# First block of a graph convolution ahead of the others, later loads on another queue, source scores from one vector, and the softmax of two target blocks ahead of the rest

## Chip, cores and metric

One core of a Trainium2 chip runs the whole program. The metric is device time in microseconds (us): the median of the runs of one kernel. The engines are named as in the profile: PE (TensorE), DVE (VectorE), ACT (ScalarE), POOL (GpSimd), and SP (SyncE), which here only issues transfers.

## What is computed

Four graph layers run one after the other on 3,125 nodes with 256 features and 100,000 edges; after each, the result is added to x and normalized by row. The change touches the first two:

```python
x = _layernorm(x + _L0_gnn_ref(x, edge_index, L0_gnn_W1, L0_gnn_W2))
x = _layernorm(x + _L1_gnn_ref(x, edge_index, edge_attr_128, Wn, bn, We, be, attn))
# layer 0, gcn_conv(x, W1), relu, gcn_conv(h, W2):
h = x @ W;  deg = segment_sum(ones, dst);  dinv = where(deg > 0, rsqrt(deg), 0)
return segment_sum(h[src] * (dinv[src] * dinv[dst])[:, None], dst)
# layer 1, attention over the edges of each target:
h = x @ Wn.T + bn;  e = edge_attr @ We.T + be
a = leaky_relu(sum((h[src] + e) * attn), 0.01)
a = exp(a - segment_max(a, dst)[dst]);  a = a / (segment_sum(a, dst)[dst] + 1e-16)
return relu(segment_sum(h[src] * a[:, None], dst))
```

Layers 2 and 3 are a gated graph layer and another convolution with a small decoder. The program works in float32; where bfloat16 is used, a float32 value is split into three bfloat16 parts.

## The kernel before

Nodes lie in 25 blocks of 128 rows (NBK). Every gather and scatter is a matrix product: for a target block b and a source block s a 128x128 "slab" holds the weights of the edges between them, and the output of b is the sum over s of slab times features. A slab is itself a product of one-hot matrices. Edges stand in a table sorted by (target block, source block, half of the target rows), up to 128 in a tile, 50 tiles for one target block (TS).

The stages, with the rows of the profile that they have:

- **Records.** dense_path first works out a row for every edge and scatters 784 groups of 128 records into the table in DRAM, with indirect DMAs on POOL's queue (L498). A record has the packed rows of source and target, two edge weights, and the edge's share of the attention score (the features times a vector made of We and attn). At the end of this stage the features H0 = dinv * (x @ W1) are split into three bfloat16 parts (L337 to L343).
- **First convolution** (pool "layer0"). For each block, load_records loads the block's records on SP (L809, tile rec_b, three buffers), casts them to source and target keys on DVE (L813 to L820), and copies the score share into q on ACT (L821). Two halves of 13 and 12 source blocks follow: onehot makes the one-hots os and od on DVE (L729), build_slab multiplies them on PE (L755) and ACT evacuates four slabs at a time (L756, PSUM in three buffers) into the bfloat16 tile wo (four buffers). apply_parts does 75 matmuls (L775). ACT scales and rectifies the sum (L838), project multiplies by W2 (two transposes L680, evacuation L681, matmuls L687), ACT scales (L841), and split writes three parts into H1 (L712 and L715 on ACT, L714 and L716 on DVE). Each slab is also written to DRAM on SP (L835).
- **Second convolution and scores.** Ten transposes turn the keys round (L850, L852), and ten writes put them into DRAM (L853). Then, for each block b: its slab is loaded on SP (L803), applied to H1 (L775), added to x with dinv (L883), normalized (norm: L696 to L704, a square root on ACT at L702), multiplied by WnT (project), bn is added to give H (L886), and the source score s1 of each node is the sum of H * attn_r over the features, plus a constant kc (L888 to L890); it is split into three parts (s1p). scores(b - 1) reads keys of the edges with that source block, broadcast to all rows (L868), compares them with the row number (L869), looks the scores up by 50 small matmuls (L871), adds them to q and takes the leaky rectifier (L874 to L877).
- **Attention.** From all of q the largest value in each target block is found: reduce (L940), transpose (L932), reduce (L934), broadcast by a matmul (L943); it is subtracted (L944) and the exponential taken (L945). For each target block weights_split splits q into three parts (L899 to L903), weighted multiplies them into the one-hots od (L909), build_slab and apply_f32 follow (L755, L783). bounds tests the spread of the scores for a flag and runs behind block 0.
- Layers 2 and 3 follow with the same helpers.

In the stages named here no order is written out by hand: a scheduler puts the instructions of each engine in an order by their place in the program, raised by a priority where one is given, and each engine then runs its own in that order. Loads of x, W2, WnT, bn and attn_r are issued from ACT's queue (L657, L666, L671); the loads of records and slabs and the writes of slabs from SP's.

Of the kernel before, what the change touches and what calls it, by code (L numbers as in the profile page):

```python
# [8 lines left out]
F32 = mybir.dt.float32  # L9
# [3 lines left out]
OP = mybir.AluOpType  # L13
# [56 lines left out]
def in_pairs(ap):  # L70

    return ap.rearrange("p n (c two) -> p n c two", two=2)
# [27 lines left out]
def dense_path(ctx: ExitStack, tc: tile.TileContext, a: dict, out: bass.AP, flag: bass.AP):  # L100
# [553 lines left out]
    nc.gpsimd.memset(x1[:, :, 0], 1.0)  # L654
    nc.gpsimd.memset(x1[:, :, D + 1], 1.0)
    x = x1[:, :, 1:D + 1]
    nc.scalar.dma_start(x, a["x_rows"])  # L657
    stats = keep.tile([P, NBK, 2], F32, name="stats")
    rstd = keep.tile([P, NBK], F32, name="rstd")
    s1 = keep.tile([P, NBK], F32, name="s1")  # L660


    def weight(pool, v, name):
        k, m = v.shape
        t = pool.tile([P, k // P, m], F32, name=name)
# [44 lines left out]
    def split(dst, src, shape):  # L710

        nc.scalar.activation(dst[0], src, AF.Copy)  # L712
        r = wk.tile(shape, F32, name="split")
        nc.vector.tensor_tensor(r, src, dst[0], op=OP.subtract)  # L714
        nc.scalar.activation(dst[1], r, AF.Copy)  # L715
        nc.vector.tensor_tensor(dst[2], r, dst[1], op=OP.subtract)  # L716

    oh = ctx.enter_context(tc.tile_pool(name="d_oh", bufs=2))

# [4 lines left out]
    until1 = ctx.enter_context(ExitStack())  # L724
    q = until1.enter_context(tc.tile_pool(name="d_q", bufs=1)).tile([P, NT], F32, name="q")

    def onehot(k, n, name, cols=P):
        t = halfslab(name, cols=cols)
        nc.vector.tensor_tensor(in_pairs(t[:, :n, :]), repeat(iota_b[:, :cols], n), pair(k, cols), op=OP.is_equal)  # L729
        return t  # L730

    def half_slabs():
# [73 lines left out]
    def load_records(b):  # L806
        ts = slice(b * TS, (b + 1) * TS)
        r = wk.tile([P, TS, 4], F32, name="rec_b", bufs=3)
        load = nc.sync.dma_start(r, trows[:, ts, :])  # L809
        for name in done:  # L810
            tc.add_manual_dep(load.ins, name, DATA, reason="it reads rows of all scatters")
        both = wk.tile([P, TS], I32, name="both")
        nc.vector.tensor_copy(both, r[:, :, 0])  # L813
# [7 lines left out]
        nc.scalar.activation(q[:, ts], r[:, :, 3], AF.Copy)  # L821


    s1p = keep.tile([P, NBK, 3], BF, name="s1p")
    with tc.tile_pool(name="layer0", bufs=1) as pool:
        W2 = weight(pool, a["L0_gnn_W2"], "W2")
        H1 = pool.tile([P, NBK, 3, D], BF, name="H1")
        for b in range(NBK):
            load_records(b)
            slab = halfslab("wo", 4)[:, :NBK, :]  # L830
            for o, n in half_slabs():
                os = onehot(cut(keys, b, o, n), n * TB, "os")
                od = onehot(cut(keyd, b, o, n), n * TB, "od", HP)
                build_slab(slab[:, o:o + n, :], b, o, n, os, [od], True)
# [3 lines left out]
            nc.scalar.activation(y, p, AF.Relu, scale=dinv[:, b:b + 1])  # L838
# [40 lines left out]
        for b in range(NBK):  # L879
            p = apply_parts(load_slab(b), H1, D)  # L880
            if b:
                scores(b - 1)
            nc.vector.scalar_tensor_tensor(x[:, b, :], p, dinv[:, b:b + 1], x[:, b, :], op0=OP.mult, op1=OP.add)  # L883
            norm(b)
            p = project(x[:, b, :], WnT, D)
            nc.vector.tensor_add(H[:, b, :D], p, bn)  # L886
            m = wk.tile([P, D], F32, name="tmp")
            nc.vector.tensor_tensor(m, H[:, b, :D], attn_r, op=OP.mult)  # L888
            nc.vector.tensor_reduce(s1[:, b:b + 1], m, axis=AX.X, op=OP.add)
            nc.vector.tensor_scalar(s1[:, b:b + 1], s1[:, b:b + 1], kc, None, op0=OP.add)  # L890
            split([s1p[:, b, i:i + 1] for i in range(3)], s1[:, b:b + 1], [P, 1])
        scores(NBK - 1)

    def weights_split(dst, tmp, w, n, bufs=1):

# [7 lines left out]
        nc.vector.tensor_copy(dst[:, 2], tw(lo))  # L903

    def weighted(oh, w3, n):
        r = []
# [19 lines left out]
    with tc.tile_pool(name="layer1", bufs=2) as pool:  # L926
        den = pool.tile([P, NBK], F32, name="den", bufs=1)

        def largest(v, n=1):

            vt = psT.tile([P, P], F32, name="tp")
            nc.tensor.transpose(vt[:n, :], v, ident)  # L932
            r = pool.tile([n, 1], F32, name=f"largest{n}", bufs=6)
            nc.vector.tensor_reduce(r, vt[:n, :], axis=AX.X, op=OP.max)  # L934
            return r
# [4 lines left out]
        nc.vector.tensor_reduce(bmax, q_by_target, axis=AX.X, op=OP.max)  # L940
        r = largest(bmax, NBK)
        c = psT.tile([P, NBK], F32, name="tp")
        nc.tensor.matmul(c, r.to_broadcast([NBK, P]), ident[:NBK, :NBK], start=True, stop=True)  # L943
        nc.vector.tensor_tensor(q_by_target, q_by_target, c[:, :, None].to_broadcast([P, NBK, TS]), op=OP.subtract)  # L944
# [885 lines left out]
```

## Time and profile before

| | us |
|---|---|
| median of 3 runs | 3448.73 |
| lowest and highest run | 3438.39 and 3451.22 |
| profiled execution, time | 3273.78 |
| profiled execution, span | 3271.9 |
| PE busy in the span | 2550.6 (78%) |
| DVE busy | 2232.4 (68%) |
| ACT busy | 921.8 (28%) |
| POOL busy | 789.0 (24%) |

The span goes from the first to the last instruction of one execution. Busy shares are means over stages with different limits; a stage is read from its own stretch of the timeline. In a row of the timeline stand start, duration, engine, line, operation, output and inputs, and the count; in brackets, how long the engine had been idle and what ended that.

### The profile page before, as it was taken

How to read it: one execution, taken by the hardware profiler on the slowest of the kernel's cores; microseconds unless marked ns; L12 is line 12 of the kernel's file. 1: busy time of each engine (PE TensorE's matmuls, PEld its weight loads, DVE VectorE, ACT ScalarE, POOL GpSimd, SP SyncE). 2: the span in 40 equal slices, each digit the busy share in tenths (PEclk: the TensorE clock that was granted, in tenths of full speed). 3: DMA queues.
4: the chain of work that ended last, by engine and by line, in shares of the span. 5: the costliest groups of instructions: out<-in, count | busy, mean ns of one | idle time of the engine just before them, and what ended most of it. 6: DMA issues, size and time to landing. Idle time of an engine off the chain costs nothing.

```text
span 3271.9 us, 60046 instructions
## 1 busy us (share of the span) xinstructions
PE 2550.6 (78%) x25737; PEld 1964.7 (60%) x25737; DVE 2232.4 (68%) x3824; ACT 921.8 (28%) x1827; POOL 789.0 (24%) x874
## 2 busy tenths in 40 slices
PE   4544443333520999999979999999999999999998
PEld 2222222222310888788868888888888767767754
DVE  8997766666773655355578888666666767767545
ACT  3332222222221444200022222222222334334321
POOL 4777777777775000000000000000000000000000
PEclk6555566666555999999989999999999999999999
DMA  4222222222212211465400000100001010010143
GB/s 138 81 78 65 70 71 71 71 71 62 79 30 59 99 72 78 165 231 217 182 2 2 2 2 2 44 15 16 16 13 19 10 13 10 10 13 9 45 138 118
DMA packets 171989, 203.46 MB, mean 62 GB/s; under 512 B 119719, under 2 KB 144796, under 8 KB 165441
## 3 DMA queue, kind: packets, MB, share of 16 engines
q1 hardware_dynamic: 134698, 188.26, 18.0%
q10 hardware_dynamic: 11927, 9.63, 1.0%
q0 software_dynamic: 25088, 1.66, 0.8%
q8 instruction: 203, 3.33, 0.4%
q14 instruction: 73, 0.60, 0.1%
HBM read 167.60 MB, written 31.86 MB: 61 GB/s over the span
## 4 chain that ended last, share of the span: by engine, by line
PE 51%; POOL 18%; DVE 17%; issue 7%; ACT 5%; DMA 2%; ACTq 0%; DVEq 0%; POOLq 0%; SPq 0%
PE acc L783 18%; POOL table L498 18%; PE acc L775 11%; PE mm L687 6%; PE slab L755 5%; DVE wo L909 4%; PE acc L1156 3%; DVE os L729 3%; PE tp L680 2%; DVE eq L465 1%; ACT L1112 1%; PE look L871 1%; ACT xT L681 1%; DVE od L729 1%; DVE rank L469 1%
## 5 line engine op out<-in xcount | busy, mean ns | idle before, releaser
L498 POOL DMA_INDIRECT table<-rec,row x784 | 757.2, 966 | 263.7 <-issue 216.9
L783 PE MATMUL acc<-x,slab_f 128*128 128x257 f32 x2500 | 592.5, 386 | 0.0
L909 DVE TENSOR_TENSOR wo<-od,w 128x1664 bf16<-128x1664 bf16 (+1 forms) x450 | 434.0, 984 | 134.8 <-PE slab L755 108.5
L783 PEld LDWEIGHTS acc<-x,slab_f 128*128 128x128 f32 x2500 | 455.8, 189 | 71.4 <-issue 5.9
L361 PE MATMUL place<-by_target,op 128*128 128x100 bf16 x392 | 40.7, 281 | 460.5 <-ACT tick L512 419.7
L775 PEld LDWEIGHTS <-wo 128*128 128x128 bf16 x3750 | 363.9, 98 | 47.9 <-issue 3.1
L755 PEld LDWEIGHTS <-os 128*128 128x128 bf16 x8750 | 296.8, 98 | 109.3 <-ACT q L821 61.4
L729 DVE TENSOR_TENSOR os<-iota_b,keys 128x3328 bf16<-128x3328 bf16 (+1 forms) x150 | 272.9, 1819 | 115.3 <-PE slab L755 114.2
L361 PEld LDWEIGHTS <-op 128*128 128x128 bf16 x392 | 33.7, 135 | 463.5 <-issue 285.3
L783 PE MATMUL acc<-features,slab_f 128*128 128x257 f32 x1250 | 297.1, 388 | 0.0
L755 PE MATMUL slab<-wo,os 128*128 128x64 bf16 x7500 | 261.1, 193 | 13.4 <-ACT slab_f L756 8.2
L783 PEld LDWEIGHTS acc<-features,slab_f 128*128 128x128 f32 x1250 | 227.9, 190 | 43.3 <-issue 12.1
L756 ACT ACTIVATE slab_f<-slab 128x512 f32<-128x512 f32 (+1 forms) x350 | 182.6, 549 | 146.0 <-PE slab L755 140.9
L775 PE MATMUL acc<-H,wo 128*128 128x256 bf16 x1875 | 218.9, 273 | 0.0
L775 PE MATMUL acc<-features,wo 128*128 128x256 bf16 x1875 | 212.9, 274 | 0.0
L1038 POOL COPY keys_t<-keys 128x2500 bf16<-128x2500 bf16 x1 | 2.5, 2520 | 721.2 <-ACT tmp L975 721.2
L512 ACT ACTIVATE tick<-place 1x1 f32<-1x1 f32 x48 | 7.7, 160 | 533.0 <-POOL tock L513 500.0
L465 DVE TENSOR_SCALAR eq<-gap 128x512 bf16<-128x512 f32 x196 | 121.8, 682 | 39.4 <-PE gap L439 39.4
L729 DVE TENSOR_TENSOR od<-iota_b,keyd 128x1664 bf16<-128x1664 bf16 (+1 forms) x150 | 147.6, 984 | 0.0
L767 PEld LDWEIGHTS <-wo 128*64 128x64 bf16 x3750 | 112.0, 110 | 47.5 <-issue 47.5
L420 PEld LDWEIGHTS <-by_target 128*52 128x52 bf16 x784 | 90.6, 138 | 77.3 <-issue 49.0
L767 PE MATMUL slab<-os,wo 128*64 128x128 bf16 x3750 | 129.6, 220 | 4.7 <-ACT slab_f L769 4.7
(286 smaller groups left out, 3621.7 us busy)
## 6 DMA issues: line engine op xcount, KB each, us to landing
ea<-in_edge_attr SPq DMA_DIRECT2D x49, 1024.0 KB
wo<-slabs SPq DMA_DIRECT2D x50, 800.0 KB
os<-rows SPq DMA_DIRECT2D x25, 832.0 KB
slabs<-wo SPq DMA_DIRECT2D x25, 800.0 KB
od<-rows SPq DMA_DIRECT2D x25, 768.0 KB
table<-rec,row POOLq DMA_INDIRECT x784, 2.1
dr<-db_row SPq DMA_DIRECT2D x48, 208.0 KB
rec_b<-table SPq DMA_DIRECT2D x75, 100.0 KB
```

Source lines behind the costliest of these rows:

```text
L420: nc.tensor.matmul(cnt[:, c + 1:, :], it["by_target"][:, c], it["by_source"][:, c:c + 1, :].to_broadcast([P, CH - c, KB]), start=False, st ...
L465: nc.vector.tensor_scalar(eq[:, 4 * g:4 * g + 4, :], of[k]["gap"][g], 0.0, None, op0=OP.is_equal)
L498: i = nc.gpsimd.indirect_dma_start(out=table, out_offset=bass.IndirectOffsetOnAxis(ap=ready[k][:, c:c + 1], axis=0), in_=rec[:, k * CH + c ...
L687: nc.tensor.matmul(p[:, :m], l, r, start=(i == 0), stop=(i == len(w) - 1))
L729: nc.vector.tensor_tensor(in_pairs(t[:, :n, :]), repeat(iota_b[:, :cols], n), pair(k, cols), op=OP.is_equal)
L755: nc.tensor.matmul(p[:, i - g, own], l, r, start=(m == 0), stop=(m == len(terms) - 1))
L756: nc.scalar.activation(dst[:, g:g + w, :], p[:, :w, :], AF.Copy)
L767: nc.tensor.matmul(p[j * HP:(j + 1) * HP, i - g, :], stat[:, i * TB + j, :], mov[:, i * TB + j, :], start=(m == 0), stop=(m == len(stats) ...
L775: nc.tensor.matmul(p[:, :m], slab[:, s, :], parts[:, s, k, :m], start=(s == 0 and k == 0), stop=(s == NBK - 1 and k == 2))
L783: nc.tensor.matmul(p[:, :m], t[:, s, :], H[:, o + s, :m], start=(o + s == 0), stop=(o + s == NBK - 1))
L909: nc.vector.tensor_tensor(in_pairs(t[:, :n, :]), in_pairs(oh[:, :n, :]), pair(w3[k], HP), op=OP.mult)
L1156: nc.tensor.matmul(acc[b][:, :3 * F0], slab[b][:, s, :], H3[:, s].rearrange("p k m -> p (k m)"), start=(s == 0), stop=(s == NBK - 1))
```

## The change

- The first block of the first convolution gets a high priority, so that the scheduler takes its records, one-hots and slab ahead of the other blocks'. The copy of the score share into q goes from ACT to POOL.
- The loads of x, WnT, bn and attn_r move from ACT's queue, at the start of the stage, to SP's queue behind block 2; that of W2 to SP's queue behind the first block's slab.
- The source score is no longer taken from H: a vector v = WnT times attn, brought to all rows (v_row), and a constant c_row = bn . attn + kc are made once; s1 is then the sum of x * v_row, plus c_row. H is made as before, but its product comes behind the score in the program.
- The last block's score and its lookup get a high priority, and its H comes behind them in the program.
- The softmax is done in two parts, target blocks 0 and 1 with a high priority, and 2 to 24 behind block 0's slabs in the program. The largest value is still that of each target block.
- Four dependencies, handed out by onehot from the list behind, make the first four one-hots of attention wait: the first for the last block's split score, the second for the first part's reduction, the next two for block 0's split weights.

```diff
-    nc.scalar.dma_start(x, a["x_rows"])
...
-    def weight(pool, v, name):
+    def weight(pool, v, name, q=nc.scalar):
...
-        nc.scalar.dma_start(t, v.rearrange("(k p) m -> p k m", p=P))
+        q.dma_start(t, v.rearrange("(k p) m -> p k m", p=P))
...
+    behind = []
+
     def onehot(k, n, name, cols=P):
         t = halfslab(name, cols=cols)
-        nc.vector.tensor_tensor(in_pairs(t[:, :n, :]), repeat(iota_b[:, :cols], n), pair(k, cols), op=OP.is_equal)
+        i = nc.vector.tensor_tensor(in_pairs(t[:, :n, :]), repeat(iota_b[:, :cols], n), pair(k, cols), op=OP.is_equal)
+        if behind:
+            tc.add_manual_dep(i.ins, behind.pop(0).ins.name, DATA, reason="what others wait for comes first")
         return t
...
-        nc.scalar.activation(q[:, ts], r[:, :, 3], AF.Copy)
+        nc.gpsimd.tensor_copy(q[:, ts], r[:, :, 3])
...
+    SOON = 20000
     with tc.tile_pool(name="layer0", bufs=1) as pool:
-        W2 = weight(pool, a["L0_gnn_W2"], "W2")
         H1 = pool.tile([P, NBK, 3, D], BF, name="H1")
         for b in range(NBK):
-            load_records(b)
...
+            with tc.high_priority(0 if b else 20000):
+                load_records(b)
+                slab = halfslab("wo", 4)[:, :NBK, :]
+                for o, n in half_slabs():
...
+                    build_slab(slab[:, o:o + n, :], b, o, n, os, [od], True)
+            if b == 0:
+                W2 = weight(pool, a["L0_gnn_W2"], "W2", nc.sync)
...
+            if b == 2:
+                WnT = pool.tile([P, KD, D], F32, name="WnT")
+                bn, attn_r = [pool.tile([P, D], F32, name=n) for n in ("bn", "attn_r")]
+                for t, v in ((x, a["x_rows"]), (WnT, a["WnT"].rearrange("(k p) m -> p k m", p=P)), (bn, row_bcast(a["L1_gnn_bn"])),
+                             (attn_r, row_bcast(a["L1_gnn_attn"].rearrange("o h c -> (o h c)")))):
+                    tc.keep_in_program_order(nc.sync.dma_start(t, v))
...
-        WnT, bn = weight(pool, a["WnT"], "WnT"), bias(pool, a["L1_gnn_bn"], "bn")
-        attn_r = bias(pool, a["L1_gnn_attn"].rearrange("o h c -> (o h c)"), "attn_r")
...
+        vc = pool.tile([P, KD], F32, name="vc")
+        for k in range(KD):
+            m = wk.tile([P, D], F32, name="tmp")
+            nc.vector.tensor_tensor(m, WnT[:, k, :], attn_r, op=OP.mult)
+            nc.vector.tensor_reduce(vc[:, k:k + 1], m, axis=AX.X, op=OP.add)
+        m = wk.tile([P, D], F32, name="tmp")
+        nc.vector.tensor_tensor(m, bn, attn_r, op=OP.mult)
+        c_row = pool.tile([P, 1], F32, name="c_row")
+        nc.vector.tensor_reduce(c_row, m, axis=AX.X, op=OP.add)
+        nc.vector.tensor_scalar(c_row, c_row, kc, None, op0=OP.add)
+        p = psM.tile([P, 512], F32, name="mm")
+        for k in range(KD):
+            nc.tensor.matmul(p[:, k * P:(k + 1) * P], vc[:, k:k + 1].to_broadcast([P, P]), ident, start=True, stop=True)
+        v_row = pool.tile([P, D], F32, name="v_row")
+        nc.scalar.activation(v_row, p[:, :D], AF.Copy)
...
-            nc.vector.scalar_tensor_tensor(x[:, b, :], p, dinv[:, b:b + 1], x[:, b, :], op0=OP.mult, op1=OP.add)
-            norm(b)
-            p = project(x[:, b, :], WnT, D)
-            nc.vector.tensor_add(H[:, b, :D], p, bn)
-            m = wk.tile([P, D], F32, name="tmp")
-            nc.vector.tensor_tensor(m, H[:, b, :D], attn_r, op=OP.mult)
-            nc.vector.tensor_reduce(s1[:, b:b + 1], m, axis=AX.X, op=OP.add)
-            nc.vector.tensor_scalar(s1[:, b:b + 1], s1[:, b:b + 1], kc, None, op0=OP.add)
-            split([s1p[:, b, i:i + 1] for i in range(3)], s1[:, b:b + 1], [P, 1])
-        scores(NBK - 1)
+            with tc.high_priority(SOON if b == NBK - 1 else 0):
+                nc.vector.scalar_tensor_tensor(x[:, b, :], p, dinv[:, b:b + 1], x[:, b, :], op0=OP.mult, op1=OP.add)
+                norm(b)
+                m = wk.tile([P, D], F32, name="tmp")
+                nc.vector.tensor_tensor(m, x[:, b, :], v_row, op=OP.mult)
+                nc.vector.tensor_reduce(s1[:, b:b + 1], m, axis=AX.X, op=OP.add)
+                nc.vector.tensor_scalar(s1[:, b:b + 1], s1[:, b:b + 1], c_row, None, op0=OP.add)
+                parted = split([s1p[:, b, i:i + 1] for i in range(3)], s1[:, b:b + 1], [P, 1])
+            if b < NBK - 1:
+                p = project(x[:, b, :], WnT, D)
+                nc.vector.tensor_add(H[:, b, :D], p, bn)
+        with tc.high_priority(SOON):
+            scores(NBK - 1)
+        p = project(x[:, NBK - 1, :], WnT, D)
+        nc.vector.tensor_add(H[:, NBK - 1, :D], p, bn)
...
-        nc.vector.tensor_reduce(bmax, q_by_target, axis=AX.X, op=OP.max)
-        r = largest(bmax, NBK)
-        c = psT.tile([P, NBK], F32, name="tp")
-        nc.tensor.matmul(c, r.to_broadcast([NBK, P]), ident[:NBK, :NBK], start=True, stop=True)
-        nc.vector.tensor_tensor(q_by_target, q_by_target, c[:, :, None].to_broadcast([P, NBK, TS]), op=OP.subtract)
-        nc.scalar.activation(q, q, AF.Exp)
+        def softmax(d0, d1):
+            qs, n = q_by_target[:, d0:d1, :], d1 - d0
+            i = nc.vector.tensor_reduce(bmax[:, d0:d1], qs, axis=AX.X, op=OP.max)
+            r = largest(bmax[:, d0:d1], n)
+            c = psT.tile([P, NBK], F32, name="tp")
+            nc.tensor.matmul(c[:, :n], r.to_broadcast([n, P]), ident[:n, :n], start=True, stop=True)
+            nc.vector.tensor_tensor(qs, qs, c[:, :n, None].to_broadcast([P, n, TS]), op=OP.subtract)
+            nc.scalar.activation(qs, qs, AF.Exp)
+            return i
+
+        with tc.high_priority(SOON):
+            i = softmax(0, 2)
+        behind += [parted, i]
...
-            weights_split(w3, wk, q[:, b * TS:(b + 1) * TS], TS, 2)
+            i = weights_split(w3, wk, q[:, b * TS:(b + 1) * TS], TS, 2)
+            if b == 0:
+                behind += [i, i]
             slab = weighted_slab(pool, b, keys, keyd, w3)
+            if b == 0:
+                softmax(2, NBK)
```

More of the change, by code (lines that the diff above doesn't have):

```diff
@@ L715, in split @@
         nc.scalar.activation(dst[1], r, AF.Copy)
-        nc.vector.tensor_tensor(dst[2], r, dst[1], op=OP.subtract)
+        return nc.vector.tensor_tensor(dst[2], r, dst[1], op=OP.subtract)
     oh = ctx.enter_context(tc.tile_pool(name="d_oh", bufs=2))
@@ L820, in load_records @@
             nc.vector.tensor_copy(k[:, ts, :], t[:, :, None].to_broadcast([P, TS, 2]))
-        nc.scalar.activation(q[:, ts], r[:, :, 3], AF.Copy)
+        nc.gpsimd.tensor_copy(q[:, ts], r[:, :, 3])
+    SOON = 20000
     s1p = keep.tile([P, NBK, 3], BF, name="s1p")
     with tc.tile_pool(name="layer0", bufs=1) as pool:
-        W2 = weight(pool, a["L0_gnn_W2"], "W2")
         H1 = pool.tile([P, NBK, 3, D], BF, name="H1")
         for b in range(NBK):
-            load_records(b)
[L830 to L834, printed above, removed]
+            with tc.high_priority(0 if b else 20000):
+                load_records(b)
+                slab = halfslab("wo", 4)[:, :NBK, :]
+                for o, n in half_slabs():
+                    os = onehot(cut(keys, b, o, n), n * TB, "os")
+                    od = onehot(cut(keyd, b, o, n), n * TB, "od", HP)
+                    build_slab(slab[:, o:o + n, :], b, o, n, os, [od], True)
+            if b == 0:
+                W2 = weight(pool, a["L0_gnn_W2"], "W2", nc.sync)
             nc.sync.dma_start(slabs[b].rearrange("p (s d) -> p s d", d=P), slab)
@@ L902, in weights_split @@
         nc.vector.tensor_tensor(lo, hi, dst[:, 1, :, 0], op=OP.subtract)
-        nc.vector.tensor_copy(dst[:, 2], tw(lo))
+        return nc.vector.tensor_copy(dst[:, 2], tw(lo))
     def weighted(oh, w3, n):
@@ L933, in largest @@
             r = pool.tile([n, 1], F32, name=f"largest{n}", bufs=6)
-            nc.vector.tensor_reduce(r, vt[:n, :], axis=AX.X, op=OP.max)
-            return r
+            nc.vector.tensor_reduce(r[:n], vt[:n, :], axis=AX.X, op=OP.max)
+            return r[:n]
         bmax = pool.tile([P, NBK], F32, name="bmax", bufs=1)
         q_by_target = q.rearrange("p (d t) -> p d t", d=NBK)
-        nc.vector.tensor_reduce(bmax, q_by_target, axis=AX.X, op=OP.max)
-        r = largest(bmax, NBK)
-        c = psT.tile([P, NBK], F32, name="tp")
-        nc.tensor.matmul(c, r.to_broadcast([NBK, P]), ident[:NBK, :NBK], start=True, stop=True)
-        nc.vector.tensor_tensor(q_by_target, q_by_target, c[:, :, None].to_broadcast([P, NBK, TS]), op=OP.subtract)
-        nc.scalar.activation(q, q, AF.Exp)
+        def softmax(d0, d1):
[10 more added lines that the diff above has]
+        behind += [parted, i]
         nc.vector.tensor_reduce(ends[:, 2:3], s1, axis=AX.X, op=OP.max)
```

## The prediction

> **What bounds the kernel now.** I first cut the span into stages (busy us of each engine in a stretch, its instructions, granted PE clock, DMA share, GB/s):
>
> ```profile
> 1041.00:1063.00 22.00, 3.97 (x58) 3.65 (x59) 10.29 (x25) 4.18 (x13) 1.16 (x3) 0.50 0.77 213
> 1063.00:1347.00 284.00, 278.98 (x3261) 245.59 (x3260) 157.75 (x253) 125.99 (x309) 0.00 (x0) 1.00 0.24 90
> 1347.00:1382.00 35.00, 28.15 (x258) 23.61 (x256) 10.73 (x27) 6.20 (x21) 0.14 (x1) 0.90 0.53 180
> 1382.00:1633.00 251.00, 247.52 (x2942) 212.88 (x2940) 138.96 (x383) 22.36 (x90) 0.00 (x0) 1.00 0.58 213
> 1633.00:1664.00 31.00, 12.21 (x188) 9.01 (x185) 21.34 (x59) 4.72 (x8) 0.00 (x0) 0.53 0.00 1
> 1664.00:2070.00 406.00, 399.42 (x5002) 345.78 (x5000) 340.51 (x573) 104.59 (x223) 1.17 (x1) 1.00 0.01 3
> ```
>
> First PE column against length: in both convolutions and in attention PE is busy 98% of the time, so a DVE or ACT instruction removed there is worth nothing. PE lacks 18 us at the first seam (scatters to first convolution), 7 us at the second, 19 us at the third (second convolution to attention). The change can win only there. The timeline of the first seam:
>
> ```profile
> 1046.43 0.20 DVE L813 CAST both<-rec_b 128x50 int32<-128x50 f32 x1 [43.46 <-DMA rec_b<-table]
> ...
> 1051.22 1.89 DVE L729 TENSOR_TENSOR os<-iota_b,keys 128x3328 bf16<-128x3328 bf16 x1
> ...
> 1059.75 0.29 ACT L821 ACTIVATE q<-rec_b 128x50 f32<-128x50 f32 x1 [7.46 <-DMA x<-in_x_rows]
> 1059.95 0.58 ACT L756 ACTIVATE wo<-slab 128x512 bf16<-128x512 f32 x1
> ...
> 1071.84 0.48 ACT L838 ACTIVATE tmp<-acc,dinv 128x256 f32<-128x256 f32 x1 [2.24 <-PE acc L775]
> ```
>
> DVE unpacks three blocks of records before the first one-hot; then ACT, in order, sits on a copy of q whose records travel behind the 3,200 KB load of x, and the first PSUM evacuation (L756) waits behind it. Block 0 is applied at 1071.84. The third seam:
>
> ```profile
> 1633.01 0.48 DVE L883 SCALAR_TENSOR_TENSOR x<-acc,dinv,x 128x256 f32<-128x256 f32 x1 [2.23 <-PE acc L775]
> ...
> 1638.48 0.66 PE L680 MATMUL tp<-ident,x 128*128 128x128 f32 x2 [4.28 <-DVE x L704]
> 1639.67 2.08 PE L687 MATMUL mm<-WnT,xT 128*128 128x256 f32 x4 [0.53 <-ACT xT L681]
> ...
> 1648.52 1.46 DVE L940 TENSOR_REDUCE bmax<-q 128x25 f32<-128x1250 f32 x1
> ...
> 1651.53 1.46 DVE L944 TENSOR_TENSOR q<-q,tp 128x1250 f32<-128x1250 f32 x1 [0.71 <-PE tp L943]
> ...
> 1656.68 1.01 DVE L909 TENSOR_TENSOR wo<-od,w 128x1664 bf16<-128x1664 bf16 x1
> ...
> 1668.95 9.38 PE L783 MATMUL acc<-features,slab_f 128*128 128x257 f32 x42
> ```
>
> One serial chain, 35.9 us from L883 to L783.
>
> **First seam.** With block 0 ahead, its five unpacking casts (0.71 us, 1046.43 to 1047.14) are followed at once by four one-hots of block 0 (1.89, 1.02, 1.75, 0.95: 5.6 us, to 1052.8). PE starts about 1050.2 instead of 1054.17, the second half follows the last one-hot, and ACT evacuates immediately, since no q copy is left on it. Slab done about 1054.3, then 72 applying matmuls; the row for 71 is 9.01 us, part of it at the slow clock, so 8.6: end 62.9, against 71.8: **-9.0 us**. Even if all 9.0 stays slow the gain is 8.4.
>
> What is late next: the built program's order (I compared both on each engine) has DVE unpack records 2 to 11 before the split of block 0's h. Rows of before: 0.71 to 0.92 us per block while DVE waits for loads, and only three record buffers; the loads of 4 and 5 wait for DVE to leave the one-hots (1052.8), block 0's slab write stands ahead of load 6. From 1059.3 on, ten blocks take to about 1067.8, while the split could start at 1066.4: ACT's second split instruction waits, with the third slab evacuation queued behind it, PE behind that: +1.1 us. Block 2's one-hots come at 1073.7, PE wants them at 1073.0: +0.8. I take **+2** (0 if records land faster, +6 if the next block's split is late too).
>
> Queues. x, WnT, bn and attn_r (3.7 MB) now stand on SP after block 2's slab write (about 1086). x took 14.8 us before (1044.08 to 1058.85); block 3's write then lands near 1110. Its buffer is one of four, wanted again by block 7 near 1130: free, and dear only if over 20 us later. x itself is first read near 1350. W2 (256 KB) stands on SP ahead of record 3: free by the same slack. The q copies on GpSimd: no row shows a 128x50 copy there; POOL's copy of one element took 188 ns, of 2,500 elements 2,520 ns, so 0.24 us each, 25 of them 6 us, beside idle POOL: 0. The rule that speaks against it is the Trainium skill's SBUF — State Buffer, "Who interferes with whom": GpSimd and a DVE instruction with two SBUF inputs exclude each other for a whole instruction. By it a copy could hold up a one-hot, up to 6 us in all, but only the 2 or 3 before 1053 delay PE: +0.5. No row of before shows it; I keep 0 with that end.
>
> Steady first convolution: PE's order changes from 15+11+24 slab matmuls around one run of 75 to runs of 24, 27 and 24, in a pattern of two blocks. Before, PE waits about 0.25 us for the transposes' input and 0.24 for xT in each block of 11.45. In the new order I find 0.1+0.1 plus 0.6 in every second block, where the second slab evacuation stands on ACT behind the two h instructions (0.47+0.42). Per pair 0.9 against 1.0: 0; with each wait 0.1 worse, 2 us; **+0.5** (-2 to +6).
>
> **Second seam.** Ten transposes with two row buffers wait for their writes (PE idle 2.17 and 4.13 us), and these stay. New: two 128x128 matmuls and one ACT copy for v_row (0.3+0.3+0.38), six DVE instructions of 0.42 on a DVE half idle. **+0.5** (-3 to +3).
>
> **Second convolution.** 0: DVE does the same number of instructions per block, PE's order is the same, period 11.14.
>
> **Third seam, step by step.** To L704 the last block now follows the steady pattern (2.35 us from L883, as 1621.87 to 1624.22): 1635.36 against 1637.92, -2.6. But the last project has not moved behind the lookup on PE: transposes and four matmuls still come first. They no longer gate the scores, which come from x by v_row: multiply, reduce, add 1635.8 to 1637.0, split to 1637.8. PE idles only 1.7 us and should stay at full clock (after 2.17 us idle, 7 matmuls took 0.93 us; after 4.13, 4 took 1.06), so the product takes 1.13, not 2.08: lookup at 1638.0 against 1644.30. DVE meanwhile waits for the product to add bn, then builds a one-hot (1.89) ahead of the sum: 1640.3; q 0.34+0.29, first reduction about 1641.2 against 1648.52: **-7.3**.
>
> The softmax of two blocks: reduce 100 instead of 1,250 elements, 0.25. But on DVE the reduction of the other 23 blocks (1.36) stands directly behind, and their subtraction (1.36) still ahead of the weights. From 1641.2: 0.2 + 1.36 + largest 0.28 + one-hot 1.0 + subtract 0.25 = 1644.25; then 0.3, second largest, 1.0 for its round over PE, 1.36: weights at 1646.9, first wo 1647.2: 6.0 us instead of 8.16: **-2.2**. ACT's table load waits for DVE in the new program; before it ran at 1644.06, nine us early. Row: 1.28 us, so exp ends at 1645.95, hidden under the subtraction. The Trainium skill, ScalarE: Activation LUTs, "What ACT_TABLE_LOAD costs", adds a drain of 1.38 us: 1647.3, then +0.4 us on the path. The row after another load (1680.38 + 1.28, sqrt at 1681.68) shows no drain; I take the row.
>
> From first wo to the applying of block 0: 12.3 us before. Now two one-hots (1.75+0.95) stand between, but PE needs 4 us (slow clock) for the first half anyway, and the last wo wait for PE's release as before: 12.5. Four matmul passes fewer remain (0.9). **-0.7**. The manual dependencies (behind) tie DVE to DVE, one in-order engine: they fix an order and add no wait. Sum of the seam -10.2 (-6 if PE is slow again and the drain is there; -13).
>
> **Sum**: -9.0 + 2 + 0.5 + 0.5 - 10.2 = -16.2 us. Profiled execution: 3273.78 (span 3271.9, 1.9 around it), to 3257.6. The timed median is 3448.73, 175 us above the profiled one; no view says where. The saved stretches are chains of fixed latencies, so I carry over the difference, rounded up to **3433** (-0.46%).
>
> **Rivals.**
> A. More: records land without delay and PE keeps its clock: 0 instead of +2.5, seam three -13, second seam -2: -24, 3425. For it: DVE's chains are short rows. Against: the in-order waits counted above. 0.30.
> B. Less: both unpacking waits occur in full (+6), cadence +4, seam three -7: about -6, 3443. For it: three record buffers and ten unpackings ahead of a split. 0.22.
> C. Slower: the new PE order in the first convolution. Each split run of the apply waits for an evacuation that stands on ACT behind h; were this 1.5 us in every block from the second on, 24 x 1.5 = 36 less 16: +20, 3469. It decides above 0.68 us per block. For it: ACT is in order, the slab PSUM has three buffers. Against: ACT busy 126 of 284 us. 0.06.
> D. The change doesn't do what it says: softmax no earlier, since the other blocks' reduction and subtraction stand ahead; seam three -8, first seam as summed: -14, 3435. It hardly differs from the forecast and is inside it.
> Forecast 0.42.
>
> About 0.5% (17 us) can be told from no change in a measurement. The forecast stands just inside it and its own spread is 8 us (3424 to 3442): half of it is counted as faster. Faster 0.43: A mostly, half of the forecast less a part; same 0.50; slower 0.07. Range for 8 in 10: 3417 to 3449, from A with its ends to B with its own.
>
> **What would show it.** ACT's first read of an applied block (L838 before) at about 1063; ACT's first slab evacuation near 1050.5; PE waits on ACT in blocks 1 and 2 of about 2 us; steady period 11.4 to 11.5. At the third seam, lookup 5 us after L883, wo at 14.2 us, apply at 26.7 (35.9 before). Attention's period stays 16.26. Wrong if the period of the first convolution rises above 11.6, the GpSimd copies show as DVE idle, or the x load delays a slab.

## The result and the profile after

| | before | changed |
|---|---|---|
| median of 12 runs, us | 3446.72 | 3450.37 |
| lowest and highest | 3438.39 and 3451.22 | 3445.60 and 3462.00 |
| profiled execution, span | 3271.9 | 3447.5 |

The ratio, of the means of the runs, is 1.0018, 95% interval 1.0009 to 1.0027: about 6 us slower (the medians are 3.7 us apart). The forecast was 3433 us, some 16 less than the 3448.73 known then.

The two profiled spans can't be set against each other. In the changed kernel's profile the last scatter of the records stage is issued at 1210.50, in that of before at 1041.15: 169 us apart in a stage that the change doesn't touch. In the experiments below the last scatter stands between 1038 and 1042 us on one chip and between 1186 and 1216 on two others, whatever the kernel, and the medians of before differ the same way (3271.63 on the first, 3436.01 and 3444.67 on the others). That also fits the 175 us between the profile of before and its timed runs, which the prediction could not place. So each run is compared with runs of before on its own chip, and inside a profile the stages are measured from the last scatter on:

| us | before | changed | difference | forecast |
|---|---|---|---|---|
| last scatter to block 0 applied (first L838, now L844) | 30.69 | 20.61 | -10.1 | -9.0 |
| from there to block 24 applied (24 periods) | 275.65 | 299.45 | **+23.8** | +2.5 |
| from there to block 2 of the second convolution (L883, now L912) | 40.27 | 41.10 | +0.8 | +0.5 |
| from there to block 24 | 245.25 | 245.30 | 0 | 0 |
| from there to the first denominator of attention (L972, now L1018) | 45.36 | 36.60 | -8.8 | -10.2 |
| from there to the end of the span | 1593.5 | 1593.9 | +0.4 | 0 |
| last scatter to end | 2230.8 | 2237.0 | +6.2 | -16.2 |

The sum of the rows, +6.2, is also what the ratio makes of 3446.72. The first and the third seam gained about what was forecast; the first convolution lost more than both together. In a second profile of the changed kernel (the last experiment) the first five rows are 21.66, 298.71, 40.22, 245.59 and 36.16 us, so a seam is known to about 1 us, and the second seam's +0.8 can't be told from 0. The stretches of the changed kernel (busy us of PE, PE's weight loads, DVE, ACT and POOL with their instructions, then granted clock, DMA share, GB/s; the stretches are the two seams and the two convolutions):

```profile
1210.50:1231.00 20.50, 11.47 (x131) 10.21 (x132) 15.82 (x46) 3.32 (x7) 6.49 (x11) 0.70 0.34 99
1231.00:1530.50 299.50, 279.10 (x3199) 237.92 (x3198) 156.83 (x234) 129.02 (x288) 9.40 (x18) 1.00 0.26 95
...
1565.50:1817.00 251.50, 247.97 (x2946) 213.22 (x2945) 141.62 (x382) 22.34 (x90) 0.00 (x0) 1.00 0.58 213
1817.00:1839.30 22.30, 12.38 (x189) 9.54 (x186) 19.02 (x47) 4.92 (x9) 0.00 (x0) 0.57 0.01 1
```

In the first convolution PE is busy 279.1 of 299.5 us, 93%, at full clock; in the second 98.6%. The same 24 periods in before:

```profile
1071.83:1347.48 275.65, 270.63 (x3193) 238.46 (x3190) 149.63 (x214) 124.38 (x304) 0.00 (x0) 1.00 0.23 88
```

PE was busy 98% of them, with as many instructions (3193 and 3199). Of the 23.8 us that are lost, 15.4 are idle time of PE (5.0 us then, 20.4 now) and 8.4 busy time: its 1,800 applying matmuls cover 213.0 us instead of 202.9, now that they run in more and shorter pieces. The timeline of the first seam:

```profile
1215.44 0.21 DVE L816 CAST both<-rec_b 128x50 int32<-128x50 f32 x1 [1.73 <-DMA rec_b<-table]
...
1216.30 1.88 DVE L730 TENSOR_TENSOR os<-iota_b,keys 128x3328 bf16<-128x3328 bf16 x1
...
1220.02 1.75 ACT L759 ACTIVATE wo<-slab 128x512 bf16<-128x512 f32 x4 [18.23 <-PE slab L758]
...
1231.11 0.47 ACT L844 ACTIVATE tmp<-acc,dinv 128x256 f32<-128x256 f32 x1 [7.03 <-PE acc L778]
```

The first one-hot comes 0.86 us after block 0's first cast (4.79 before), ACT's first evacuation (L759, now of four slab groups in a row) 4.6 us after that cast (13.5 before), and no copy of q stands on ACT. Block 0 is applied 20.61 us after the last scatter. The third seam:

```profile
1816.96 0.48 DVE L912 SCALAR_TENSOR_TENSOR x<-acc,dinv,x 128x256 f32<-128x256 f32 x1 [3.50 <-PE acc L778]
...
1820.82 2.07 PE L686 MATMUL mm<-WnT,xT 128*128 128x256 f32 x4 [0.53 <-ACT xT L680]
...
1825.99 1.51 DVE L977 TENSOR_REDUCE bmax<-q 128x2 f32<-128x100 f32 x2
...
1828.86 1.28 ACT L982 ACT_TABLE_LOAD   x1 [7.30 <-DVE q L981]
...
1830.15 0.29 ACT L982 ACTIVATE q<-q 128x100 f32<-128x100 f32 x1
1830.27 1.35 DVE L981 TENSOR_TENSOR q<-q,tp 128x1150 f32<-128x1150 f32 x1 [0.71 <-PE tp L980]
...
1831.91 1.02 DVE L942 TENSOR_TENSOR wo<-od,w 128x1664 bf16<-128x1664 bf16 x1
...
1845.02 8.51 PE L786 MATMUL acc<-features,slab_f 128*128 128x257 f32 x38
```

From the last block's result at 1816.96, the first reduction comes 9.03 us later (15.51 before), the first weighted one-hot 14.95 (23.67), the applying run 28.06 (35.94; 12 of the 50 matmuls stand ahead of it, 8 before).

What is new stands in the middle of the first convolution. Each applying of 75 matmuls is broken up, and each piece begins with a wait:

```profile
1371.78 0.66 PE L758 MATMUL slab<-od,os 128*128 128x64 bf16 x17
1372.21 0.42 ACT L711 ACTIVATE H<-tmp 128x256 bf16<-128x256 f32 x1
...
1372.54 1.06 ACT L759 ACTIVATE wo<-slab 128x512 bf16<-128x512 f32 x2
...
1373.17 2.84 PEld L778 LDWEIGHTS <-wo 128*128 128x128 bf16 x27 [0.77 <-ACT wo L759]
...
1376.13 0.86 PE L758 MATMUL slab<-od,os 128*128 128x64 bf16 x24
1376.56 1.57 ACT L759 ACTIVATE wo<-slab 128x512 bf16<-128x512 f32 x3 [2.49 <-PE slab L758]
...
1377.21 3.83 PEld L778 LDWEIGHTS <-wo 128*128 128x128 bf16 x36 [0.34 <-ACT wo L759]
```

Twenty slab matmuls (the row of 17 and three single ones behind it) and then 24 are followed directly by the applying matmuls that read these very slabs. ACT starts on the first four slabs only as these are done and takes 0.59 us for each four; PE's weight loads idle 0.34 us where ACT is free, and 0.77 where the split of h (L711) is ahead on ACT. A block in before:

```profile
1199.95 1.25 ACT L756 ACTIVATE wo<-slab 128x512 bf16<-128x512 f32 x3
...
1201.07 0.86 PE L755 MATMUL slab<-od,os 128*128 128x64 bf16 x24
...
1201.70 0.59 ACT L756 ACTIVATE wo<-slab 128x512 bf16<-128x512 f32 x1
1201.77 8.35 PE L775 MATMUL acc<-features,wo 128*128 128x256 bf16 x75
...
1202.49 1.09 ACT L756 ACTIVATE wo<-slab 128x512 bf16<-128x512 f32 x2
```

There too, by the built program, the applying reads the slab of its own block, but it begins with the first half (39 matmuls), and that half was evacuated (1199.95) while PE multiplied by W2 and built the second half (1201.07). The second half is evacuated (1201.70 and 1202.49) under the applying of the first: PE waits for neither. The waits added up over the 24 periods (engine, line, what it waited for, us in all, times, longest), first the changed kernel, then before:

```profile
PEld L778 <- ACT wo L759: 22.9, 47, 0.8
PE acc L778 <- ACT wo L759: 17.2, 47, 0.7
...
PEld tp L679 <- ACT tmp L844: 6.6, 24, 0.3
PEld mm L686 <- ACT xT L680: 6.5, 24, 0.3
```

```profile
PEld tp L680 <- ACT tmp L838: 6.2, 24, 0.5
PEld mm L687 <- ACT xT L681: 5.1, 22, 0.2
```

The waits for the transposes are there in both. The waits for wo, 22.9 us in 47 places, two in each block, were not there before; they are nearly all of the 23.8 us. (PE's own rows show 17.2 of it as idle; in the rest the matmuls ahead of a wait are still running.)

### The profile page after: what moved, and what is told of

Its sections match the earlier page's. It is cut to its first block, busy times and chain, and to the rows that moved or that the text cites. A ratio compares the mean times of both kernels' runs of the same rounds, so it can differ in the third digit from the quotient of the medians.

```text
span 3447.5 us, 60077 instructions
## 1 busy us (share of the span) xinstructions
PE 2560.0 (74%) x25744; PEld 1962.8 (57%) x25744; DVE 2241.9 (65%) x3834; ACT 924.1 (27%) x1804; POOL 801.5 (23%) x899
## 4 chain that ended last, share of the span: by engine, by line
PE 49%; another core or an unknown queue 19%; DVE 16%; ACT 10%; issue 4%; DMA 1%; POOL 1%; ACTq 0%; SPq 0%; DVEq 0%; POOLq 0%
PE acc L786 17%; PE acc L778 11%; PE mm L686 6%; PE slab L758 4%; DVE wo L942 3%; PE acc L1202 3%; DVE os L730 3%; ACT dT L453 2%; ACT away L452 2%; PE tp L679 2%; DVE eq L465 1%; ACT L1158 1%; PE look L899 1%; PE place L361 1%
## 5 line engine op out<-in xcount | busy, mean ns | idle before, releaser
L778 PEld LDWEIGHTS <-wo 128*128 128x128 bf16 x3750 | 360.6, 98 | 72.8 <-ACT wo L759 22.9
L778 PE MATMUL acc<-features,wo 128*128 128x256 bf16 x1875 | 221.9, 273 | 17.2 <-ACT wo L759 17.2
L759 ACT ACTIVATE slab_f<-slab 128x512 f32<-128x512 f32 (+1 forms) x350 | 182.7, 548 | 143.7 <-PE slab L758 138.5
L482 DVE TENSOR_TENSOR sel<-place,by_source 128x400 f32<-128x400 f32 (+1 forms) x52 | 28.4, 547 | 210.0 <-PE place L361 192.3
```

Source lines behind the costliest of these rows:

```text
L759: nc.scalar.activation(dst[:, g:g + w, :], p[:, :w, :], AF.Copy)
L778: nc.tensor.matmul(p[:, :m], slab[:, s, :], parts[:, s, k, :m], start=(s == 0 and k == 0), stop=(s == NBK - 1 and k == 2))
```

## The experiments

Theory: the loss is PE's order in the first convolution, and the order comes from the priority contexts around blocks 1 to 24. They have an offset of 0, so they look like nothing. But the scheduler restores its counter when a context ends. Printed while the program is built, the counter around block 1's records, one-hots and slab is

```
               at entry   behind the block
with context      5224        5224
without any       5294        5364
```

With the context, the applying of a block has numbers that begin where those of its slab begin, not behind them. It competes with the second half of its own slab, and PE takes it as soon as the first half is evacuated. Rivals: the copies of q on GpSimd, the 3.7 MB of loads on SyncE's queue, or block 0's priority.

**Context for block 0 alone.** Run twice, on two chips.

```diff
-            with tc.high_priority(0 if b else 20000):
+            with (nullcontext() if b else tc.high_priority(20000)):
```

> The changed kernel, with the priority context entered for block 0 alone; the other blocks are not inside one. Theory (the context with offset zero around the other blocks is what makes PE break up its applying): the period of the first convolution is 11.45 us again, PE waits inside the applying are gone, seam gains of about 10 and 9 us stay: 17 to 18 us less than before, ratio 0.995. Rival 1 (the q copies on GpSimd, the 3.7 MB of loads on SyncE's queue or the early block 0 cost the time): the period stays at 12.3 to 12.6 us, ratio 1.002. Rival 2 (both): period near 12, ratio 0.998.

> The same kernel as e1_block0_only, as a comparison for the next on the same chip. Expected as there: ratio to before 0.994 to 0.9945.

Ratio 0.9942 (0.9929 to 0.9956), 3251.91 us against 3271.63; the second time 0.9945 (0.9927 to 0.9964). First convolution 274.97 us, its periods 11.38 to 11.50. The waits of PE's weight loads, over the same 24 periods:

```profile
PEld tp L679 <- ACT tmp L844: 5.9, 24, 0.2
PEld mm L686 <- ACT xT L680: 5.4, 24, 0.2
```

None is for wo. GpSimd's copies, the loads and block 0's priority are all still there, so none of them alone is the cause.

**The contexts alone, in the kernel before.**

```diff
-            load_records(b)
-            slab = halfslab("wo", 4)[:, :NBK, :]
+            with tc.high_priority(0):
+                load_records(b)
+                slab = halfslab("wo", 4)[:, :NBK, :]
...
```

> The kernel before, with nothing changed but a priority context of offset zero around the records, one-hots and slab of every block of the first convolution. Theory: the period rises from 11.45 to about 12.4 us, 24 periods: 21 to 24 us more than before, ratio 1.0065; the seams stay as they were. Rival 1 (an offset of zero is nothing, the time comes from other parts of the change): ratio 1.000.

Ratio 1.0074 (1.0060 to 1.0087), 24 us more. First convolution 298.55 us (22.9 more), third seam 45.52; block 0 is applied at 33.11 us, 2.4 later, which was not expected. The wait is there, with the same size:

```profile
PEld L775 <- ACT wo L756: 23.4, 48, 0.8
```

So the contexts are sufficient for the loss, without any other part of the change, and the first experiment shows that they are needed for it. The change has 24 contexts of offset 0 in the second convolution too, around each block's norm and score. There the period stayed at 11.14 us (245.30 us against 245.25 for 22 blocks): what costs time is the order that comes of a context, not the context.

**The order held on PE, contexts kept.**

```diff
+                if after:
+                    tc.add_manual_dep(i.ins, after.ins.name, DATA, reason="the whole slab comes first")
...
-            p = apply_parts(slab, H0, D)
+            p = apply_parts(slab, H0, D, last)
```

> The changed kernel as it is, with one dependency more in each block of the first convolution: its first applying matmul stands behind the last matmul of its slab, both on PE. It adds no wait, only an order. Theory (it is PE's order, and nothing else that the contexts move, that costs the time): as with the context for block 0 alone, period 11.45, ratio 0.995. Rival (what the contexts move on DVE, ACT or SyncE, or contention of the copies and loads, costs the time): period stays above 12, ratio 1.000 to 1.002.

Ratio 0.9956 (0.9942 to 0.9969), first convolution 276.60 us, its periods 11.49 to 11.56. One order on PE, that the 75 matmuls stand behind the block's own slab, takes back 22.9 of the 23.8 us with the contexts in place. So the loss goes through PE's order. The scheduler plans the other engines around it, though: DVE's wait for ACT's half of h, 102.9 us in the changed kernel's first convolution, is 8.2 here and 8.1 with the context for block 0 alone. What DVE's order does by itself was not tried.

**The third seam alone.** First convolution, its loads and the copies of q as before (the edit against the changed kernel, without the loads).

```diff
-            with tc.high_priority(0 if b else 20000):
-                load_records(b)
+            load_records(b)
...
-        nc.gpsimd.tensor_copy(q[:, ts], r[:, :, 3])
+        nc.scalar.activation(q[:, ts], r[:, :, 3], AF.Copy)
```

> The first convolution, its loads and its q copies as before; only the scores by one vector, the priority of the last block and the softmax in two parts are kept. Theory (the two ends are independent): third seam 36.6 us from the last block's result to the first block's denominator (45.4 before), second seam 0.8 us more, first convolution 11.45 us a period: 8 us less, ratio 0.9977. Rival (a gain here needs the early first convolution, or is given back in layers 1 to 3): ratio 1.000.

Ratio 0.9974 (0.9964 to 0.9985), 8.4 us less; third seam 36.53 us, first convolution 275.63, as before. The second seam is 42.12, 1.9 more where 0.8 was expected. The third seam's gain doesn't need the first's.

**What gains at the first seam.** Two versions of the kernel with the context for block 0 alone: one with the q copies back on ACT, one with the loads back on ACT's queue.

```diff
-        nc.gpsimd.tensor_copy(q[:, ts], r[:, :, 3])
+        nc.scalar.activation(q[:, ts], r[:, :, 3], AF.Copy)
```

> The changed kernel with the priority context for block 0 alone (as in e1_block0_only), and the q copies back on ACT; the loads stay on SyncE's queue. Theory A (the stall at the first seam was ACT waiting for records that travelled behind x; with x gone the copies wait for little): block 0 applied at most 1 us later than in e1_block0_only (20.5 us after the last scatter), ratio to before 0.994 to 0.995. Theory B (it is the copies themselves in ACT's in-order queue): block 0 applied 4 to 9 us later, ratio 0.996 to 0.997.

Block 0 is applied at 20.25 us, as with the copies on GpSimd: theory A. Ratio 0.9934 (0.9908 to 0.9959). But the second and third period take 11.99 and 12.68 us, since ACT again waits for records behind the first two blocks (its timeline):

```profile
1219.56 0.29 ACT L824 ACTIVATE q<-rec_b 128x50 f32<-128x50 f32 x1 [3.98 <-DMA rec_b<-table]
...
1230.89 0.29 ACT L824 ACTIVATE q<-rec_b 128x50 f32<-128x50 f32 x1 [4.29 <-DMA rec_b<-table]
```

```diff
+    nc.scalar.dma_start(x, a["x_rows"])
...
+        W2 = weight(pool, a["L0_gnn_W2"], "W2")
```

> As e1_block0_only, with the loads of x, W2, WnT, bn and attn_r back on ACT's queue at the start of the stage; the q copies stay on GpSimd. Theory A (ACT no longer waits for records, so x may travel early; but in the built order the first three blocks' records are unpacked again ahead of the first one-hot): first one-hot 4.8 us after the first records instead of 0.9, block 0 applied about 24.5 us after the last scatter, ratio to before 0.9955. Theory B (x in the way of the records is the whole loss): block 0 applied at 29 to 31 us as before, ratio 0.997.

Ratio 0.9953 (0.9935 to 0.9970); block 0 applied at 25.73 us:

```profile
1191.32 0.20 DVE L817 CAST both<-rec_b 128x50 int32<-128x50 f32 x1 [14.37 <-DMA rec_b<-table]
...
1196.01 1.99 DVE L731 TENSOR_TENSOR os<-iota_b,keys 128x3328 bf16<-128x3328 bf16 x1
...
1199.79 1.75 ACT L760 ACTIVATE wo<-slab 128x512 bf16<-128x512 f32 x4 [9.57 <-PE slab L759]
...
1211.86 0.47 ACT L844 ACTIVATE tmp<-acc,dinv 128x256 f32<-128x256 f32 x1 [7.96 <-PE acc L779]
```

Theory A again, 1.2 us later than expected: the first one-hot comes 4.69 us after the first cast, three blocks being unpacked ahead of it although block 0 has its priority; ACT evacuates as soon as PE delivers. So the 10 us have two halves: 5.0 from an ACT that doesn't wait for records behind x, 5.2 from the place of the loads, with which the scheduler changes the order on DVE (3.8 of them lie ahead of the first one-hot). Moving the loads alone brings both at block 0 and gives 1.8 us back in the next blocks. And with the loads and copies moved, the priority brings nothing: without any context in the first convolution the built program is the same, instruction for instruction, as with the one for block 0.

**A version for the third seam.** In the changed kernel the last projection, the other blocks' reduction and subtraction, and the bounds still stand ahead of the first weighted one-hot. Here they are ordered behind it, each by a dependency within its own engine; the second version has an early exponential too.

```diff
+                    tc.add_manual_dep(t_.ins, held[0].ins.name, DATA, reason="the first softmax comes first")
...
-                softmax(2, NBK)
+                softmax(2, NBK, wlast[0])
...
+                if b == NBK - 1:
+                    nc.scalar.activation(late_p.tile([P, 1], F32, name="early"), rstd[:, b:b + 1], AF.Exp)
```

> As e1_block0_only, with four orders more at the third seam, each by a dependency within one engine: the last block's projection behind the first softmax's matmuls on PE, its sum with bn and the softmax of blocks 2 to 24 and the bounds behind block 0's last weighted one-hots on DVE. Theory (in the changed kernel these stood ahead of what the first slab waits for): from the last block's result to the first denominator 33 to 34 us instead of 36.6, ratio to before 0.9932 to 0.994. Rival (the time only moves behind the first slab, since DVE is the next limit there): 35 to 37 us, ratio 0.994 to 0.995.

Ratio 0.9927 (0.9904 to 0.9950), third seam 33.56 us. But from the last scatter to the end it is 2210.4 us, against 2210.3 and 2210.7 in the two runs of the context for block 0 alone. Of the 1.7 us gained at the seam, 1.1 are given back behind the first denominator (1595.2 us to the end against 1594.0 to 1594.1): the rival is largely right.

> As e7_seam3_reordered, and an exponential of one element per partition right behind the last square root, so that the activation table is loaded before the first softmax needs it. Theory: 1.28 us of table load come off the chain between subtraction and exponential: 1.0 to 1.4 us less than e7_seam3_reordered, ratio to before about 0.993. Rival (the load was hidden, or the early one delays the score's split on ACT): no less, or 1 us more.

> The same kernel as e8_seam3_table_early. Theory: third seam 32 us, 3.3 us less than in e10_block0_again in the profile and 3 to 4 us less in the median, ratio to before about 0.993. Rival (given back behind the first slab): no less than e10_block0_again.

Ratio 0.9924 (0.9900 to 0.9948), then 0.9944 (0.9927 to 0.9961). Third seam 31.96 us, 31.94 in the repetition, 3.3 less than with the context alone; the early exponential is worth 1.6. The timeline:

```profile
1777.61 0.49 DVE L915 SCALAR_TENSOR_TENSOR x<-acc,dinv,x 128x256 f32<-128x256 f32 x1 [3.17 <-PE acc L781]
...
1779.75 1.28 ACT L922 ACT_TABLE_LOAD   x1
...
1785.17 0.26 DVE L941 TENSOR_REDUCE bmax<-q 128x2 f32<-128x100 f32 x1
...
1787.70 0.29 ACT L948 ACTIVATE q<-q 128x100 f32<-128x100 f32 x1 [5.49 <-DVE q L947]
...
1788.39 1.02 DVE L974 TENSOR_TENSOR wo<-od,w 128x1664 bf16<-128x1664 bf16 x1
...
1788.88 2.07 PE L688 MATMUL mm<-WnT,xT 128*128 128x256 f32 x4 [0.53 <-ACT xT L682]
```

The table is loaded while DVE normalizes, and the exponential starts 0.10 us after the subtraction ends. From last scatter to end 2209.5 and 2208.5 us: 1 to 2 us less than with the context alone. The 3 to 4 us less that were expected in the median are not there (3425.4 with the early exponential, 3424.1 with the context alone, on one chip): the runs of one kernel spread over 6 to 10 us. Both beat before and the change; whether the extra orders are worth anything stays open.

**The changed kernel once more,** on the chip of the last comparison.

> The changed kernel itself, beside the two versions below on one chip. Theory (the loss is 24 periods of about 1 us, whatever the length of the records stage on the chip): ratio to before 1.0015 to 1.0025, first convolution 299 us from the first applied block to the last. Rival (the length of the first convolution follows the chip): other than 299 us.

Ratio 1.0018 (1.0009 to 1.0027), first convolution 298.71 us.

## Why the prediction was wrong

- **First seam, -9.0: right.** -10.1, and -9.0 in the repetition, by the steps that were named. "ACT evacuates immediately, since no q copy is left on it" and the four one-hots in a row are in the timeline. But the four one-hots come first because the loads moved, not because of the priority that was said to bring them: that part of the forecast was right by luck.
- **"What is late next", +2: not there.** With the contexts gone the first three periods are 11.39 us each, and the first convolution is 0.7 us shorter than before. The records landed in time. (In the changed kernel the first period is 13.41 us and 12.66 in the repetition, where the later ones are 12.3 to 12.7.)
- **Steady first convolution, "+0.5 (-2 to +6)": the step that failed.** The new order of PE was seen, but the sum of its waits was mis-sized: 0.9 us in each pair of blocks against 1.0 before, 0 in all. By the waits of PE's weight loads above a pair had (6.2 + 5.1) / 12 = 0.9 us before and has (22.9 + 6.6 + 6.5) / 12 = 3.0 now. The 2.1 between them account for the growth of a pair, from 22.9 to 24.9 us. Two terms were wrong. A wait for wo was charged once in a pair, 0.6 us, where ACT has h ahead of the evacuation; there are four, 0.77 + 0.34 + 0.46 + 0.34 = 1.9 us, and ACT is free in the last three, which were put at nothing. And the waits for the transposes and xT, taken to fall to 0.1 us each, stayed at 0.27. The rows of before had the pieces: an evacuation takes 0.59 us and can start only behind its slab matmuls. There the evacuation of each half of a slab ran under PE's work on the other half. The new order took that cover away, and the question "what hides this now" was asked of every edit but not of this one.
- **Rival C** had the right place, with 1.5 us in each block and a chance of 0.06; 1.0 was measured, above the 0.68 from which it decides. Its reason, an evacuation that stands on ACT behind h, holds for one of the four waits. It was set aside because ACT is busy for less than half of the time. That is no argument: the other three waits are there with ACT free.
- **GpSimd against DVE.** A copy took 1.97 us beside a one-hot of 1.88, and two one-hots of block 0 took 1.09 and 1.82 us against 1.02 and 1.75, 0.14 us in all. That agrees with the Trainium skill (SBUF — State Buffer, "Who interferes with whom"), by which the two exclude each other, but it is the copy that waits. The prediction gave this +0.5 us as its end; the 0 that it kept was nearly right.
- **Second convolution, 0: right.** Second seam, +0.5: +0.8, and 0 in the repetition, so it can't be told.
- **Third seam, -10.2: right in the mechanism,** -8.8 here and -10.1 in the version with the context for block 0 alone. First reduction -6.5 against -7.3: the product took 2.07 us and not 1.13, since PE's clock fell ahead of it (below); where it fell later, with the context for block 0 alone, the reduction came 7.4 us earlier. Softmax to first weighted one-hot 5.9 us against 6.0. From there to the denominator 0.7 us were to be gained and none was (21.7 us both times). "ACT's table load waits for DVE" is the row at 1828.86, and the load is hidden under the subtraction at 1830.27, as was said. The exponential starts 1.29 us behind the start of the load. The Trainium skill (ScalarE: Activation LUTs, "What ACT_TABLE_LOAD costs") adds a drain of 1.38 us to the load; this trace shows none.
- Nothing shows a loss in the loads on SyncE's queue: with the context for block 0 alone the periods stay between 11.38 and 11.50 us throughout.

Without the one failed term the forecast is met within its spread: with the context for block 0 alone it is 20.4 us less in the profile from the last scatter on and 19.7 in the median, against 16.2 forecast; the 4 us more are mostly the +2 and +0.5 that did not come.

## What to carry to other kernels

A scheduling context is not neutral because its offset is 0: enter it only for what it is meant for, and compare the order of the engine that sets the end before and after. On an engine that is busy 98% of the time, put other work of that engine between a producer and the consumer of its output, where a second engine stands between the two: half a slab of matmuls was enough here. Placed directly behind, each piece pays the latency over the other engine, here twice in each of 24 blocks, which is more than two seams of 10 us. Measure from a mark inside the profile when chips differ in a stage that the change doesn't touch.

## What was unexpected of the hardware

PE's clock fell after a short idle time. Two stretches of the changed kernel at the third seam (columns as above; the clock is third from the end):

```profile
1816.00:1819.80 3.80, 2.16 (x59) 1.99 (x56) 2.41 (x10) 0.20 (x1) 0.00 (x0) 1.00 0.01 2
1819.80:1822.90 3.10, 2.49 (x13) 1.74 (x14) 1.58 (x7) 0.79 (x3) 0.00 (x0) 0.58 0.00 0
```

PE idles 1.72 us from 1818.16 to 1819.88, behind a time at full clock that ends with 50 lookups of three columns, and four matmuls that took 1.13 us in the steady state (1370.48) took 2.07. In before it was idle 2.17 us at the second seam, and the next seven matmuls took 0.93 us, as if at full clock. So the length of the gap alone doesn't tell, though the prediction took it for the measure. With the context for block 0 alone the same instructions stand at the third seam (a row of the timeline at the product, then two stretches):

```profile
1622.35 0.41 PE L679 MATMUL tp<-ident,x 128*128 128x128 f32 x2 [1.72 <-DVE x L703]
...
1623.29 1.13 PE L686 MATMUL mm<-WnT,xT 128*128 128x256 f32 x4 [0.53 <-ACT xT L680]
```

```profile
1623.20:1624.20 1.00, 0.91 (x4) 0.68 (x4) 0.69 (x5) 0.45 (x3) 0.00 (x0) 1.00 0.00 0
1624.20:1625.70 1.50, 1.50 (x52) 1.40 (x50) 1.26 (x3) 0.00 (x0) 0.00 (x0) 0.55 0.04 11
```

The same gap of 1.72 us, behind the same lookups, and the product is done at full clock in 1.13 us; the clock falls behind it. If the means of 0.58 and 0.55 are made of full and half speed, it fell 3.3 us behind the last block's result in the changed kernel (about 1820.3) and 4.9 us behind it here (about 1624.35). Of the eight profiles that have this sequence, the product took 2.07 us in four and 1.13 in four. The Trainium skill (TensorE: Matmul & The Clock Gate, "Part 1: The HAM clock gate") ties the clock to how busy PE was in a free-running window of about 3.4 us. That would fit, if such a window ended at another point of the program in each run, and 1 us of the third seam would then hang on where it ended. It isn't shown: all four short products are in versions with the context for block 0 alone.

GpSimd's copies of 128x50 elements, minimum, median and maximum in ns:

```profile
L824 POOL COPY q<-rec_b x25: 252/314/1966, 1215.8 to 1252.7; 128x50 f32<-128x50 f32 x25
```

Beside the one-hots a copy took up to 1.97 us, six times its median, while a one-hot lost 0.07 us (three of the first six took 1.09, 1.82 and 1.10 us, against 1.02, 1.75 and 1.02): where the two meet, nearly all of the delay is in GpSimd's records.

The records stage took 1038 to 1042 us on one chip and 1186 to 1216 on others, with the same instructions. No run here says why.
